# Third block of a four-block transformer: routing each token to two of four experts by an on-chip sort

## The chip, the cores and the metric

The kernel runs on one core of a Trainium2 chip. The metric is the device time of one execution in microseconds (us); 1322.86 us is the median of three runs before the change. Engines are named as the profile names them: PE (TensorE matmuls; PEld its weight loads), DVE (VectorE), ACT (ScalarE), POOL (GpSimd), SP (SyncE, which here only issues DMAs). A line number such as L1105 is a line of the kernel before.

## The reference, cut to what matters

The input is 32 sequences ("batches") of 128 tokens with 144 channels, float32. A transformer block, a rotation per sequence, a second transformer block and a third one follow one another. The third block is attention and then a mixture of four experts, of which each token uses the two with the largest gate logits:

```python
h = _modulate(_ln(x), sh_msa, sc_msa)
...                                                   # attention, 16 heads of 9 channels
x = x + g_msa[:, None, :] * o
xf = _modulate(_ln(x), sh_mlp, sc_mlp).reshape(-1, C)  # 4096 tokens, C = 144
gate_logits = xf @ w_gate                              # 4 experts
topk_logits, topk_idx = jax.lax.top_k(gate_logits, 2)
gates = jax.nn.softmax(topk_logits, axis=-1)
cw = jnp.sum(jax.nn.one_hot(topk_idx, 4) * gates[..., None], axis=1)
hmid = jax.nn.gelu(jnp.einsum('tc,ech->eth', xf, w1) + b1[:, None, :], approximate=True)  # 576 wide
eo = jnp.einsum('eth,ehc->etc', hmid, w2) + b2[:, None, :]
return x + g_mlp[:, None, :] * jnp.einsum('te,etc->tc', cw, eo)
```

## The kernel before

All of x stays in SBUF (`x_sb`). The order of the instructions on every engine is written out by hand. Time is cut into ticks: in each tick one batch of a layer enters its attention, and the main loop at L1344 emits three stages of three neighbouring batches (`scores`, `weigh`, `project_out`) with named gaps "a", "e", "t", "stats", "b0", "b", "den", "pre1", "c", "y1", "y2", "y3", "z", "d" between them. `put(tick, gap, f, ...)` hangs any other work into a gap; `put2` puts the two halves of a generator into two gaps. Batches go in groups of four (G), eight groups per layer; layer l starts at tick first[l] = 0, 35, 67. Each engine executes its instructions in the order in which the loop emitted them, so a gap fixes an instruction's place on its engine.

In the third block, for group n with t0 = 67 + 4n, the layer norm of a batch is transposed by `ln_T` into `hM_m` (128 channels) and `hR_m` (16 channels and a constant, in four copies of 32 rows). `gate_logits` is at tick t0+7; `expert_ranks` and `expert_weights` at t0+8 make `cw`, four weights per token, two of them zero. Then every expert is computed for every token:

- `moe1` (through `fc1` and `both`, matmuls at L665) multiplies the 512 tokens of a group, as the moving operand, by chunks of 128 hidden columns. Two experts are a pair of 9 chunks (`PAIRS`); the last 64 columns of both share chunk `SHARED`. Gelu is at L964, into `hid`.
- `shared_by_gate` (L1093, L1094) multiplies the shared chunk by the two gate weights.
- `moe2_parts` (L1105, L1110) multiplies `hid` of one batch by the second weights, 4 products per batch and expert and one for the shared chunk; L1114 and L1116 on DVE add the result, times the gate weight, to `acc`.
- `moe_bias` (L1076, L1078, on POOL) starts `acc` with the experts' biases; `moe_out` (L1121, L1122, on POOL) multiplies by the gate of the block, adds to `x_sb`, and L1123 stores the group.

A group's experts take ticks t0+8 to t0+12. Attention of the last batch ends with tick 100; what is left of groups 6 and 7 follows it with no attention beside it. Weights of the third block's first pair are loaded once by `load_late`, of the second by the `load_pair` at L1329. SP also loads the gates of each group (L305), several ticks ahead.

Of the kernel before, what the change touches and what calls it, by code (L numbers as in the profile page):

```python
# [8 lines left out]
F32 = mybir.dt.float32  # L9
U32 = mybir.dt.uint32  # L10
I32 = mybir.dt.int32
# [17 lines left out]
PAIR_COLS = NPC * (256 + C)  # L29
# [3 lines left out]
NG = B // G  # L33
EPS = 1e-6
# [32 lines left out]
def tile_kernel(ctx: ExitStack, tc: tile.TileContext, a: dict, out: bass.AP):  # L67
# [43 lines left out]
    hid = const.tile([128, NPC, G, T], F32, name="hid")  # L111
    prep = ExitStack()
# [906 lines left out]

    def gate_logits(g):  # L1020
# [13 lines left out]
    def expert_ranks(g):  # L1034
# [5 lines left out]
        cw = small.tile(sh, F32, tag="cw", name=f"cw_{g[1]}", bufs=2)  # L1040
# [11 lines left out]
        nc.vector.tensor_scalar(rank, rank, 1.5, None, ALU.is_lt)  # L1052
# [4 lines left out]
    def expert_weights(g):  # L1057
        lg, (cw, rank, one) = gr[g].pop("lg"), gr[g]["cw"]
        nc.scalar.activation(lg, lg, AF.Exp)
        nc.vector.tensor_tensor(cw, lg, rank, ALU.mult)  # L1060
        nc.vector.tensor_reduce(one, cw, AX.X, ALU.add)
        nc.vector.reciprocal(one, one)
        nc.vector.tensor_tensor(cw, cw, one.to_broadcast([128, G, E]), ALU.mult)
        gr[g]["cw"] = cw

    def moe_bias(g, i):

        if i == 0:
            gr[g]["acc"] = late.tile([128, G, C], F32, tag="acc", name=f"acc_{g[1]}", bufs=2)
        acc = gr[g]["acc"][:, i, :]  # L1070
        for e in range(E):
            w = gr[g]["cw"][:, i, e : e + 1]
            t = acc
            if e:
                t = late.tile([128, C], F32, tag="bias", name=f"bias_{g[1]}_{i}_{e}", bufs=2)
            nc.gpsimd.tensor_scalar(t, L3.b2[:, e, :], w, 0.0, ALU.mult, ALU.add)  # L1076
            if e:
                nc.gpsimd.tensor_tensor(acc, acc, t, ALU.add)  # L1078

    def moe1(g, pair, part, rest_first):  # L1080
        to = ((0, 1, 2), (SHARED, 3, 4), (5, 6, 7))[part]
        return fc1(g, PAIRS[pair], f"3_{g[1]}_{pair}", 3 * part, to, rest_first)

    def shared_by_gate(g, pair):


        cwx = late.tile([128, G, 2, 64], F32, tag="cwx", name=f"cwx_{g[1]}_{pair}", bufs=1)
        cw = gr[g]["cw"][:, :, 2 * pair : 2 * pair + 2]
        nc.gpsimd.tensor_copy(cwx, cw.unsqueeze(3).to_broadcast([128, G, 2, 64]))
        yield  # L1090
# [5 lines left out]
    def moe2(g, e, i):  # L1096
        for _ in moe2_parts(g, e, i):
            pass
# [456 lines left out]
```

## Time and profile before

| | |
|---|---|
| three runs | 1322.86, 1318.93, 1335.67 us |
| profiled execution | 1327.05 us, its span 1325.3 us |
| granted PE clock | 0.991 of full |
| busy in the span | PE 1266.7, ACT 832.9, DVE 799.8, POOL 699.9 us |
| tick 75, the first with expert work (batch 6 in `weigh`) | 841.8 us |
| last projection of attention (`project_out` of the last batch) | issued at 1250.3 us, done by 1250.9 us |
| last matmul of the experts ends / store issued / span ends | 1318.7 / 1322.0 / 1325.3 us |

A row of the list of groups reads: line, engine, operation, output<-input by the program's names, shapes, count | busy us, mean ns of one | idle time of that engine just before them and what ended it. A row of windows gives start:end, length and then each engine's busy time with the number of instructions. The chain of waits lists start, us, and the piece of work that the end waited for. A float32 product appears as two matmul passes (a single 128x128 transpose as one). The times of the profile are those of one execution; 1322.86 is the median of the others.

### The profile page before, as it was taken

The page shows a single profiled execution, that of the slowest core. Times are in us where ns is not written, and L with a number is a line of the kernel's source. Part 1 is how long each engine was busy: PE and PEld are TensorE (multiplying, and loading weights), DVE is VectorE, ACT ScalarE, POOL GpSimd, SP SyncE. Part 2 cuts the span into 40 slices and gives each one's busy share as a digit, 9 for nine tenths or more (in the row PEclk, how much of TensorE's full clock was granted, in tenths as well). Part 3 has the DMA queues.
Part 4 walks back from the last instruction along what each step waited for, and adds up shares of the span by engine and source line. Part 5 has one row for each costly group of instructions (what it writes and reads, how often), then busy time and mean ns, then how long its engine had stood idle before and what let it go on. Part 6 is the DMA issues. An engine that isn't in the chain of part 4 may idle for free.

```text
span 1325.3 us, 35652 instructions
## 1 busy us (share of the span) xinstructions
PE 1266.7 (96%) x14180; PEld 923.5 (70%) x14180; DVE 799.8 (60%) x2516; ACT 832.9 (63%) x1832; POOL 699.9 (53%) x1691
## 2 busy tenths in 40 slices
PE   6989898999999989999999999999999999999997
PEld 5668686786776566677776766667676767677665
DVE  5698988866764355666566667545454546455322
ACT  2568767678767555686767777756565656555431
POOL 5667777756744343445445445736363636351632
PEclk9999999999999999999999999999999999999999
DMA  9200000000003000000110000201000000000000
GB/s 229 61 2 21 20 3 18 20 3 22 20 13 121 18 11 20 11 20 10 45 29 14 17 20 11 75 11 19 10 19 11 19 11 19 10 19 2 19 9 9
DMA packets 21671, 34.43 MB, mean 26 GB/s; under 512 B 2304, under 2 KB 12448, under 8 KB 21248
## 3 DMA queue, kind: packets, MB, share of 16 engines
q1 hardware_dynamic: 20848, 31.70, 8.0%
q8 instruction: 114, 1.87, 0.6%
q10 hardware_dynamic: 656, 0.42, 0.2%
q14 instruction: 53, 0.43, 0.1%
HBM read 29.65 MB, written 2.47 MB: 24 GB/s over the span
## 4 chain that ended last, share of the span: by engine, by line
PE 69%; DVE 4%; ACT 1%; issue 1%; POOL 0%; POOLq 0%; DVEq 0%
PE ps_h L665 19%; PE ps_f L1105 9%; PE ps_s L853 6%; PE ps_qk L665 6%; PE ps_o L880 5%; PE ps_w L853 5%; PE ps_f L970 4%; PE ps_pj L944 3%; PE ps_v L665 2%; DVE nm L858 2%; PE ps_f L1110 1%; PE ps_o L812 1%; PE ps_cw L1093 1%; PE ps_hT_m L652 1%; PE ps_hT_m L653 1%; PE ps_z L1002 1%
## 5 line engine op out<-in xcount | busy, mean ns | idle before, releaser
L858 DVE TENSOR_REDUCE nm<-ps_s 128x4 f32<-128x512 f32 x384 | 246.4, 682 | 96.9 <-PE ps_w L853 79.3
L865 ACT ACTIVATE pr<-ps_w 128x512 f32<-128x512 f32 x384 | 208.6, 595 | 107.6 <-PE ps_w L853 106.0
L853 PE MATMUL ps_w<-q,kT 32*128 32x128 f32 x3072 | 228.6, 283 | 0.2 <-ACT hid L964 0.2
L853 PE MATMUL ps_s<-kT,qT 32*128 32x256 f32 x1536 | 227.9, 404 | 0.7 <-ACT kT L788 0.6
L853 PEld LDWEIGHTS ps_w<-q,kT 32*128 32x128 f32 x3072 | 193.3, 186 | 9.7 <-issue 6.2
L964 ACT ACTIVATE hid<-ps_h 128x512 f32<-128x512 f32 (+1 forms) x224 | 119.1, 591 | 108.9 <-PE ps_h L665 108.5
L853 PEld LDWEIGHTS ps_s<-kT,qT 32*128 32x128 f32 x1536 | 134.9, 184 | 30.0 <-issue 9.2
L665 PE MATMUL ps_h<-hM_m,mlps 128*128 128x512 f32 x304 | 146.3, 615 | 0.0
L1114 DVE SCALAR_TENSOR_TENSOR acc<-ps_f,cw,acc 128x144 f32<-128x144 f32 x128 | 46.6, 366 | 152.3 <-PE ps_f L1110 73.6
L930 POOL TENSOR_TENSOR x_sb<-x_sb,res_a 128x144 f32<-128x144 f32 x96 | 47.0, 489 | 151.2 <-DVE res_a L933 149.9
L880 PE MATMUL ps_o<-pr,vaug 128*32 128x128 f32 x3072 | 104.9, 277 | 0.8 <-issue 0.8
L880 PEld LDWEIGHTS ps_o<-pr,vaug 128*32 128x32 f32 x3072 | 78.7, 110 | 34.3 <-PE ps_w L853 20.0
L665 PEld LDWEIGHTS ps_h<-hM_m,mlps 128*128 128x128 f32 x304 | 53.9, 191 | 66.2 <-issue 65.0
L731 POOL TENSOR_SCALAR kT<-kT,cst 128x512 f32<-128x512 f32 x40 | 62.3, 1563 | 61.6 <-ACT kT L718 60.6
L970 PE MATMUL ps_f<-mlps,hid 128*128 128x144 f32 x640 | 93.2, 293 | 0.0
L970 PEld LDWEIGHTS ps_f<-mlps,hid 128*128 128x128 f32 x640 | 82.5, 191 | 7.3 <-issue 3.4
L865 ACT ACT_TABLE_LOAD x57 | 73.1, 1283 | 8.0 <-PE ps_w L853 7.2
L626 POOL TENSOR_SCALAR rs_m_a<-mv_m_a 128x2 f32<-128x2 f32 x81 | 15.5, 191 | 116.6 <-DVE mv_m_a L624 88.2
L655 ACT ACTIVATE hM_m<-ps_hT_m,modM 128x128 f32<-128x128 f32 x96 | 44.6, 465 | 49.1 <-PE ps_hT_m L653 49.0
L961 ACT ACT_TABLE_LOAD x58 | 74.4, 1283 | 1.0
L930 POOL TENSOR_TENSOR x_sb<-x_sb,res_m 128x144 f32<-128x144 f32 x64 | 32.3, 510 | 80.0 <-DVE res_m L933 79.9
L1105 PEld LDWEIGHTS ps_f<-pair,hid 128*128 128x128 f32 x512 | 66.9, 190 | 8.4 <-issue 7.7
(324 smaller groups left out, 2963.5 us busy)
## 6 DMA issues: line engine op xcount, KB each, us to landing
gates<-gates SPq DMA_DIRECT2D x48, 288.0 KB, 3.5
x_sb<-in_x SPq DMA_DIRECT2D x8, 288.0 KB, 9.4
out_x<-x_sb SPq DMA_DIRECT2D x8, 288.0 KB, 2.5
mlps<-in_L_mlp SPq DMA_DIRECT2D x2, 1000.0 KB, 6.1
pair<-in_L_mlp SPq DMA_DIRECT2D x1, 1800.0 KB, 9.5
mlps<-in_L_mlp SPq DMA_DIRECT2D x1, 1800.0 KB, 8.2
pow<-in_W SPq DMA_DIRECT2D x4, 320.0 KB, 7.7
mlps<-in_L_wmod SPq DMA_DIRECT2D x4, 290.0 KB, 4.9
```

The lines of the kernel that those rows point to most:

```text
L665: nc.tensor.matmul(ps, x, y, start=k == 0, stop=k == 1)
L731: eng.tensor_scalar(o, k, m, None, ALU.mult)
L853: nc.tensor.matmul(o, x, y, start=True, stop=True)
L858: nc.vector.tensor_reduce(nmv[:, at0 : at0 + 2, ONE : ONE + 2], view.rearrange("p (r t k) -> p r t k", t=2, k=T), AX.X, ALU.max, negate=True,)
L865: nc.scalar.activation(pr[:, 4 * e : 4 * e + 4, :].rearrange("p s q -> p (s q)"), view, AF.Exp, scale=SCALE,)
L880: nc.tensor.matmul(po[rows4(j), t, :], v[:, 4 * j + 2 * t + r, :], prs[j // 2][:, 4 * (j % 2) + 2 * r + t, :], start=r == 0, stop=r == 1,)
L930: nc.gpsimd.tensor_tensor(x_sb[:, b, :], x_sb[:, b, :], t, ALU.add)
L961: nc.scalar.activation(t, half, AF.Gelu_apprx_tanh)
L964: nc.scalar.activation(hid[:n, i], ps[:n], AF.Gelu_apprx_tanh)
L970: nc.tensor.matmul(ps, hid[:, at0, i, :], w2[:, m, :], start=m == 0, stop=m == NFC - 1)
L1105: nc.tensor.matmul(ps[:, 0, :], hid[:, at0 + m, i, :], w2[:, at0 + m, :], start=m == 0, stop=m == 3)
L1114: nc.vector.scalar_tensor_tensor(acc, ps[:, 0, :], w, acc, ALU.mult, ALU.add)
```

## The change

Each token's normalised row is written to DRAM, a sort on the chip gives every (token, choice) pair a slot in tiles of 128 slots, each tile belonging to one expert, and only these tiles are multiplied. Groups are sorted in five sets of 1, 1, 2, 2 and 2 groups (`SETS`). A set of one group has 11 tiles, of two groups 19: twice its number of batches, and 3 for the tiles that experts fill only in part. The count is fixed, whatever the routing: 79 tiles in all, in 42 pairs (37 of two tiles, 5 of one).

- `token_rows`: two transposes, a DVE copy and a store of 128 rows of 1 KB to `sets[k].x`, for each batch.
- `places`: counts, offsets and slot numbers, in steps that are put into the gaps of one tick: DVE instructions with matmuls between them, ending in `S.expert` (a tile's expert), `S.take` (token of each slot) and `S.give` (where its result goes). Slots without a token go to a dump area.
- `fetch`: an indirect DMA on POOL gathers the 128 rows of a tile. `fetch_w`: SP reads the tile's expert into a register and loads that expert's first weights and the last 64 rows of the second with three DMAs from a computed address.
- `turned`, `expert1`, `expert2`: transposes of the gathered rows, the first product with gelu, the second product. In `expert2` PE reads the expert into a register and takes the second weights, as the moving operand, from a computed address in `exp_w2` (four experts, loaded once).
- `give`: an indirect DMA on POOL scatters a tile's 128 result rows of 576 B to `sets[k].y`. `fetch_y` loads both results of every token of a batch; `combine` weighs and adds them (DVE), multiplies by the gate and adds to `x_sb` (POOL), and stores two batches.
- `put_sets` replaces the placing of `moe1`, `moe2` and the rest: set k is sorted at tick ready, and its first ("f") and second ("s") products go one after the other into three slots per tick ("b0", "pre1", "y2"), stretched over the ticks until the next set begins; the last set has one unit per slot from tick 105.

Gone are `moe_bias`, `shared_by_gate`, `moe1`, `moe2_parts`, `moe_out` and the loads of the pairs. The gate logits and the ranking stay, with a few more DVE instructions. The core of the diff:

```diff
+SETS = ((0,), (1,), (2, 3), (4, 5), (6, 7))
...
+    row_bufs = [hid_flat[:, 2304 + 256 * i : 2560 + 256 * i] for i in range(3)]
+    xg_bufs = [hid_flat[:, 3072 + 256 * i : 3328 + 256 * i] for i in range(6)]
+    h_bufs = [hid_flat[:, 1152 * i : 1152 * i + 1152] for i in range(2)]
...
+    def token_rows(s):
+        layer, b, g, i = of(s)
+        k, j = set_of[g[1]]
+        ps = bank([128, 2, 128], f"ps_row_{s}")
+        nc.tensor.transpose(ps[:, 0, :], gr[g]["hM_m"][:, i, :], ident)
+        nc.tensor.transpose(ps[:, 1, :], gr[g]["hR_m"][:, i, :], ident)
+        row = row_bufs[b % 3]
+        nc.vector.tensor_copy(row, ps.rearrange("p a c -> p (a c)"))
+        at0 = (j * G + i) * T
+        nc.sync.dma_start(sets[k].x[at0 : at0 + T], row)
...
-    def moe_bias(g, i):
-        if i == 0:
-            gr[g]["acc"] = late.tile([128, G, C], F32, tag="acc", name=f"acc_{g[1]}", bufs=2)
-        acc = gr[g]["acc"][:, i, :]
...
+    def places(k):
+        S = sets[k]
+        nb, nt = S.nb, S.nt
+        ps = bank([128, 9, E], f"ps_pre_{k}")
+        nc.tensor.matmul(ps[:, : nb + 1], K.lower, S.sel[:, : nb + 1], start=True, stop=False)
+        ones = cst[:, K_ONES : K_ONES + 1].to_broadcast([128, 128])
+        for b in range(nb):
+            nc.tensor.matmul(
+                ps[:, b + 1 : nb + 1], ones,
+                S.sel[:, b : b + 1].to_broadcast([128, nb - b, E]), start=False, stop=b == nb - 1,
+            )
...
+        for q in range(nb // 2):
+            hot = work.tile([128, 4, 128], F32, tag=("xM", "xR")[q % 2], name=f"hot_{k}_{q}", bufs=1)
+            ps = bank([128, 19], f"ps_slots_{k}_{q}")[:, :nt]
+            for i in range(4):
+                at0 = 4 * q + i
+                nc.vector.tensor_scalar(
+                    hot[:, i], K.iota, hilo[:, 1, at0 : at0 + 1], None, ALU.is_equal
+                )
+            for i in range(4):
+                nc.tensor.matmul(ps, hot[:, i], tv[:, 4 * q + i], start=i == 0, stop=i == 3)
...
+    def fetch(k, t):
+        S = sets[k]
...
+        S.xg[t] = xg_bufs[n_taken["x"] % 6]
...
+        nc.gpsimd.indirect_dma_start(
+            S.xg[t], None, S.x[:, :],
+            bass.IndirectOffsetOnAxis(ap=S.take[:, t : t + 1].bitcast(U32), axis=0),
+        )
+    def fetch_w(k, j):
+        S = sets[k]
...
+        slot = mlps[:, 3 * FF * (n % 2) : 3 * FF * (n % 2 + 1)]
+        half_ = mlps[:, 6 * FF + C * (n % 3) : 6 * FF + C * (n % 3 + 1)]
+        S.w1[j] = slot, half_
+        for u, t in enumerate(tiles_of(k, j)):
+            e = nc.values_load(
+                S.expert[:, t : t + 1], engines=(mybir.EngineType.SP,), min_val=0, max_val=E - 1
+            )
+            rows = slice(64 * u, 64 * u + 64)
+            nc.sync.dma_start(
+                slot[:, FF * u : FF * u + FF], a["L3_w1"][bass.ds(e * 128, 128), :]
+            )
+            nc.sync.dma_start(
+                slot[rows4(u), 2 * FF : 3 * FF], a["L3_w1R"][bass.ds(e * 32, 32), :]
+            )
+            nc.sync.dma_start(half_[rows], a["L3_w2h"][bass.ds(e * 64, 64), :])
+    def turned(k, j):
+        S = sets[k]
+        n = len(tiles_of(k, j))
+        ps = bank([128, 4, 128], f"ps_X_{k}_{j}")
+        for u, t in enumerate(tiles_of(k, j)):
+            x = S.xg.pop(t)
+            nc.tensor.transpose(ps[:, 2 * u], x[:, :128], ident)
+            nc.tensor.transpose(ps[:, 2 * u + 1], x[:, 128:], ident)
+        S.xT = late.tile([128, 4, 128], F32, tag="xT", name=f"xT_{k}_{j}", bufs=1)
+        nc.scalar.copy(S.xT[:, : 2 * n], ps[:, : 2 * n])
+    def expert1(k, j):
+        S, xT = sets[k], sets[k].xT
+        ts = list(enumerate(tiles_of(k, j)))
+        slot, half_ = S.w1.pop(j)
+        psa = [bank([128, 4, 128], f"ps_H_{k}_{t}") for u, t in ts]
+        psc = bank([128, 128], f"ps_Hc_{k}_{j}")
+        for u, t in ts:
+            for m in range(4):
+                at0 = FF * u + 128 * m
+                nc.tensor.matmul(
+                    psa[u][:, m], slot[:, at0 : at0 + 128], xT[:, 2 * u], start=m == 0, stop=False
+                )
+        for u, t in ts:
+            at0 = FF * u + 512
...
+        for m in range(5):
+            at0 = 2 * FF + 128 * m
+            for u, t in ts:
+                rows = rows4(u)
+                o, n = (psa[u][:, m], 128) if m < 4 else (psc[64 * u : 64 * u + 64], 64)
+                nc.tensor.matmul(
+                    o, slot[rows, at0 : at0 + n], xT[rows, 2 * u + 1], start=False, stop=m >= 3
+                )
...
+        for u, t in ts:
+            nc.scalar.activation(
+                H[:, 512 * u : 512 * u + 512], psa[u].rearrange("p m t -> p (m t)"),
+                AF.Gelu_apprx_tanh,
+            )
...
+    def expert2(job):
+        k, j, half_, H, ts = job
+        S = sets[k]
+        at = [
+            nc.values_load(
+                S.expert[:, t : t + 1], engines=(mybir.EngineType.PE,), min_val=0,
+                max_val=E - 1,
+            ) * EXP2_COLS
+            for u, t in ts
+        ]
+        ps = [bank([128, C], f"ps_Y_{k}_{t}") for u, t in ts]
+        def w(at0, u):
+            return exp_w2[:, at0 : at0 + (E - 1) * EXP2_COLS + C][:, bass.ds(at[u], C)]
+        for u, t in ts:
+            for m in range(4):
+                at0 = 512 * u + 128 * m
+                nc.tensor.matmul(
+                    ps[u], H[:, at0 : at0 + 128], w(C * m, u), start=m == 0, stop=False
+                )
+        for u, t in ts:
+            rows = slice(64 * u, 64 * u + 64)
+            nc.tensor.matmul(ps[u], H[rows, 1024:1152], half_[rows], start=False, stop=True)
...
+        for u, t in ts:
+            nc.vector.tensor_copy(y[:, u], ps[u])
+        for u, t in ts:
+            to_give.append((k, t, y, u))
...
+    def give():
...
+        nc.gpsimd.indirect_dma_start(
+            S.y[:, :], bass.IndirectOffsetOnAxis(ap=S.give[:, t : t + 1].bitcast(U32), axis=0),
+            y[:, u], None,
+        )
+    def fetch_y(s):
...
+        y = work.tile([128, 2, C], F32, tag="qkraw", name=f"y_{s}")
+        nc.sync.dma_start(
...
+    def combine(g, i0):
+        cwT, n = gr[g]["cwT"], g[1]
+        k, j = set_of[n]
+        S = sets[k]
+        ps = [bank([128, C], f"ps_b2_{n}_{i0 + i}") for i in range(2)]
+        for i in range(2):
+            rows = slice(32 * (i0 + i), 32 * (i0 + i) + E)
+            nc.tensor.matmul(ps[i], cwT[rows], b2[rows], start=True, stop=True)
+        for i in range(2):
+            s = 2 * B + n * G + i0 + i
+            b, at0 = n * G + i0 + i, j * G + i0 + i
...
+            nc.vector.scalar_tensor_tensor(
+                acc, acc, S.w[:, at0, 0:1], ps[i], ALU.mult, ALU.add
+            )
+            nc.vector.scalar_tensor_tensor(
+                acc, y[:, 1], S.w[:, at0, 1:2], acc, ALU.mult, ALU.add
+            )
+            nc.gpsimd.tensor_tensor(acc, acc, gr[g]["gm"][:, i0 + i, :], ALU.mult)
+            nc.gpsimd.tensor_tensor(x_sb[:, b, :], x_sb[:, b, :], acc, ALU.add)
+        b = n * G + i0
+        nc.sync.dma_start(out[b : b + 2].rearrange("b t c -> t b c"), x_sb[:, b : b + 2, :])
...
-                for pair in range(2):
-                    at_ = t0 + 8 + 2 * pair
-                    put2(at_, "stats", "b0", moe1, g, pair, 0, True)
-                    put2(at_, "den", "pre1", moe1, g, pair, 1, False)
-                    put2(at_ + 1, "stats", "b0", moe1, g, pair, 2, True)
-                    put2(at_, "stats", "y1", shared_by_gate, g, pair)
-                    put2(at_, "y2", "y3", moe2_parts, g, 2 * pair, 0)
-                    put(at_ + 1, "b", moe2, g, 2 * pair, 1)
-                    put(at_ + 1, "c", moe2, g, 2 * pair, 2)
-                    put(at_ + 1, "y2", moe2, g, 2 * pair, 3)
-                    for i in range(G):
-                        put(at_ + 2, "aabb"[i], moe2, g, 2 * pair + 1, i)
...
+    units = []
+    for k, ns in enumerate(SETS):
+        ready = first[2] + G * ns[-1] + 8
+        end = first[2] + G * SETS[k + 1][-1] + 10 if k + 1 < len(SETS) else None
+        nt = 2 * G * len(ns) + 3
+        pairs = (nt + 1) // 2
+        units.append((ready, end, nt, pairs))
...
+        for k, (ready, end, nt, pairs) in enumerate(units):
+            for gap in ("b0", "pre1") + ("c", "y2") * (G * len(SETS[k]) // 4) + ("z",):
+                put(ready, gap, lambda k=k: sets[k].steps())
+            mine = [u for u in order if pairs_[u[1]][0] == k]
+            q0 = max(q, len(SLOTS) * (ready + 2))
+            room = None if end is None else len(SLOTS) * end - q0
+            for i, u in enumerate(mine):
+                q = when[u] = q0 + (i if room is None else i * room // len(mine))
...
+        for u in order:
+            J, at_ = u[1], when[u]
+            k, j = pairs_[J]
+            if u[0] == "f":
+                if J == 0:
+                    put(*slot_of(at_ - 1), turned, k, j)
+                put(*slot_of(at_), first_product, J)
+                if J + 1 < len(pairs_):
+                    put(*slot_of(max(at_, when["f", J + 1] - 1)), turned, *pairs_[J + 1])
+            else:
+                put(*slot_of(at_), lambda J=J: expert2(jobs.pop(J)))
+                for i in range(1, 3):
+                    put(*slot_of(at_ + i), give)
+                if J + 3 < len(pairs_):
+                    fetches(J + 3, at_)
+                if j == units[k][3] - 1:
+                    done = at_ // len(SLOTS) + 2
+                    for i, nn in enumerate(SETS[k]):
+                        g = 2, nn
+                        put(done + i, "den", gate_bias, g)
+                        for i0 in (0, 2):
+                            for ii in range(2):
+                                put(done + i, ("b", "y1")[i0 // 2], fetch_y, 2 * B + nn * G + i0 + ii)
+                            put(done + i, ("c", "z")[i0 // 2], combine, g, i0)
+                        need_gm[done + i - 1].append(nn)
...
```

## The prediction

> **What bounds the kernel now.** The page's busy times were read first, then busy time by windows, then the chain of waits in one group of the third block, then its end. The windows run from tick 75 (first expert work) to the last projection of attention, and from there to the last matmul; the columns are start:end, length, busy PE, PEld, DVE, ACT, POOL, clock, DMA.
>
> ```profile
> PE 1266.7 (96%) x14180; PEld 923.5 (70%) x14180; DVE 799.8 (60%) x2516; ACT 832.9 (63%) x1832; POOL 699.9 (53%) x1691
> ...
> 841.80:1250.90 409.10, 408.65 (x3908) 290.39 (x3906) 210.28 (x631) 239.15 (x453) 210.26 (x428) 1.00 0.06 17
> 1250.90:1318.70 67.80, 67.72 (x389) 45.52 (x387) 18.84 (x61) 20.36 (x44) 20.53 (x44) 1.00 0.02 5
> ...
> 957.00:1022.50 65.50, 65.50 (x633) 46.54 (x637) 34.17 (x104) 38.85 (x75) 34.67 (x69) 1.00 0.05 15
> ```
>
> PE has no gap in either stretch; 65.5 us is one group, four ticks. So the third block lasts as long as PE's work: what leaves PE is gained, and any new wait of PE costs in full. The chain within that group gives the shares, and pieces of it give prices:
>
> ```profile
> 958.00 2.77 PE ps_h L665 x6
> 960.77 0.98 PE ps_f L1105 x8
> ...
> 1264.37 0.11 PE ps_hT_m L652
> ...
> 1238.13 0.88 PE ps_w L853 x16
> ```
>
> A float32 product is two passes. A pass of 512 columns is 2.77/6 = 0.46 us, of 144 columns 0.98/8 = 0.122, of 128 columns 0.11; where two products use different 32-row strips they run side by side, 0.88/16 = 0.055 a pass. In the group's chain the experts hold 32.9% (ps_h) + 24.6% + 3.2% (ps_f, L1105 and L1110) + 1.8% (ps_cw) = 62.5%, 40.9 us; eight groups make 327 us, of which 68 lie after attention and 259 before. Attention and the rest are 24.6 us a group.
>
> **PE's work after.** First product of a pair of tiles: 16 passes x 0.11 = 1.76, the half chunk 4 x 0.055 (two column halves) = 0.22, the 16 extra channels 20 x 0.055 = 1.10; transposes 4 x 0.11 = 0.44; second product 16 x 0.122 + 0.25 = 2.21. That is 5.73 us a pair; a lone tile, without a neighbour, 3.65. 37 and 5 of them: 230 us. `token_rows` 64 x 0.11 = 7; sorts (25 products for a two-group set, 13 for one group, two passes each at about 0.1) 3 x 5 + 2 x 2.6 = 20; biases 5. Sum 262 against 327: only 65 us less, since 128 full tile products became 79, but small moving operands and extra work take part of it back.
>
> Where it lies decides. By tick 100 `put_sets` has emitted sets 0 to 2 (65 + 55 us) and ten of the twenty units of set 3 (30), with rows 7, sorts 15 and biases 3: 175 us against 259, **-84** before the end of attention. The other 87 us come after it, where 68 were.
>
> **What is added to PE before attention ends.** Ticks 75 and 76 lose their filler, since set 0 starts at 77: attention alone is 6.15 us, but neighbouring ticks of the second block are never below 8.0 apart: **+4**.
>
> `expert2` reads two registers and computes eight addresses on PE's sequencer. One such load is in the trace:
>
> ```profile
> L585 SPq TENSOR_LOAD <-more x1: 500/500/500, 246.7 to 246.7; - x1
> L585 SPq FUSED_REGOPS  x1: 188/188/188, 247.3 to 247.3; - x1
> L585 SPq SEQ_ASSERT  x1: 29/29/29, 247.5 to 247.5; - x1
> L585 PEldq TENSOR_LOAD <-more x1: 488/488/488, 318.9 to 318.9; - x1
> ```
>
> Two loads with their register steps are 2 x (0.49 + 0.19 + 0.03) = 1.42 us, eight addresses 8 x 0.19 = 1.52: 2.94 us a pair when nothing hides it. But the load at 318.9 ran while matmuls in front of it started as late as 322.0: the sequencer was 3 us ahead, which would hide it all. PE's semaphore steps in the third block stand 0 to 3 us ahead of their matmuls, with 0.65 in the middle. So 0 to 2.94; I take **0.8** a pair, nearer to hidden: 26 second products, +21.
>
> Sort steps put DVE work and the matmuls that need it into one gap: 12 such steps for sets 0 to 3. PE waits while DVE finishes two score reductions (0.68 each, L858) and four one-hot rows (about 0.25 each), 2.4 us if bare; half of it is taken: 15. The bias products share banks with DVE work that waits for `fetch_y`: 8 times about 1.2, 10. Bounds 0 and 50; **+25**.
>
> POOL: of its 34.7 us a group, the expert work is 16 x 0.39 + 12 x 0.49 (L1076, L1078) + 1.2 + 2.9 = 16; that goes. `combine` adds 8 x 0.49. Then 9.9 gathers and 9.9 scatters a group, of which no row exists. Nearest rows: SP's plain DMA issue, 0.39, and POOL's own longest operation, 1.56 (L731).
>
> ```profile
> L1123 SPq DMA_DIRECT2D out_x<-x_sb x8: 388/389/389, 915.1 to 1322.0; - x8
> ...
> DMA to landing us min/median/max: 2.4/2.5/3.1
> ...
> L731 POOL TENSOR_SCALAR kT<-kT,cst 128x512 f32<-128x512 f32 x40 | 62.3, 1563 | 61.6 <-ACT kT L718 60.6
> ```
>
> I take c = 1.3, nearer to the latter, because 128 rows have to be addressed one by one: POOL 22.3 + 19.8 x 1.3 = 48 us of a group that lasts about 60. Hidden, but the layer norms queue behind gathers and scatters on POOL, and their transposes on PE are late: **+10** (0 to 80, see the rival). ACT stays near 40 us a group (fewer columns of gelu, one more copy a pair), DVE near 35; both hidden. SP moves some 400 KB a tile, 4 MB a group: in 60 us that is below what the first slices of the page show (229 GB/s).
>
> Sum before attention ends: -84 + 4 + 21 + 25 + 10 = **-24**.
>
> **The end.** Before, 1250.9 to 1325.3 is 74.4 us: 67.8 of packed matmuls, DVE 0.4, POOL 1.40 + 1.39, the store and its landing. After, three parts.
>
> First, the rest of set 3: 25 us of products, sort 5, logits 1, registers 5, so 36. Meanwhile the last group passes through norm, row store (2.5), logits, ranks, the whole sort (some 25 small DVE steps at 0.2, 16 one-hot rows) and the first gather (1.3 + 2.5) before its first product can start: about 34 us in series. Both are in the same in-order queues and don't overlap perfectly: 45.
>
> Second, set 4, one unit per slot with nothing beside it: 55 + 8 for registers = 63. Here the order of the built program adds a wait: each scatter waits until the scatter before it into the same DRAM tile has landed, and POOL stands still meanwhile, with the next gathers behind it. Two scatters a pair are 2 x (1.3 + 2.5) = 7.6 us against PE's 6.5: about 8 in all. SP issues six loads a pair, 2 x (0.72 + 3 x (0.19 + 0.39)) = 4.9 us and some 3 to landing, into two slots used in turn: a load has from one first product to the next but one, about 9 us, and just fits. Those that stand on SP behind the stores of set 3, which wait for POOL, come late: 4. Sum 75 (55 to 100).
>
> Third, the close: copy 0.3, last scatter 3.8, then four rounds, because on SP each store stands in front of the next `fetch_y`: load 3.0, DVE 2 x 0.37, POOL 4 x 0.49 = 5.7 each; last store 2.9. Sum 30, where 6 were.
>
> 45 + 75 + 30 = 150, **+76**. Net -24 + 76 = **+52** on 1325.3. The profiled execution, 1327.05, stands 4.2 over the median, so the forecast is 1322.9 + 52 = 1375 us.
>
> [...]
>
> ```profile
> 450.00:460.00 10.00, 8.81 (x59) 5.23 (x60) 3.41 (x8) 3.94 (x7) 1.88 (x9) 0.83 0.00 0
> ...
> 451.19 0.36 PE L812 MATMUL ps_nm<-cst,nm 128*128 128x128 f32 x1 [1.38 <-DVE nm L858]
> ```
>
> The granted clock sank to a mean of 0.83 after an idle stretch of only 1.38 us. [...]
>
> **Rivals.** *The work is hidden after all (faster).* One mechanism: PE's sequencer and queues run far enough ahead. For it: PE busy for 408.65 of 409.10 us, the 3 us lead at L585. Against: the end has nothing to hide behind. Without registers (-34), sort waits (-25), POOL lateness (-10), and with an end whose parts overlap (-22), it is 1284. It passes below 1296 once these exposures stay under about 12 us of my 91. *POOL becomes the bound.* At c above (60 - 22.3)/19.8 = 1.9 us POOL outlasts PE. At 2.5 a group takes 72: +74 - 10, and 2 x 5.0 a pair in the end, +26: 1465. For it: serial scatters; against: longest POOL row 1.56. *Registers bare.* 2.94 instead of 0.8 a pair: 42 x 2.1 = +88: 1463. For it: eight computed addresses in 2 us of matmul; against: the lead.
>
> **How the numbers follow.** Forecast 0.48 (its own range 1325 to 1425), hidden 0.26, POOL 0.13, registers 0.13. The range reaches to both sides' bounds, 1290 to 1460. Two per cent, about what a measurement can tell from no change, is 1296 to 1349: from hidden 0.20 faster and 0.06 same, from the forecast 0.07 same; the rest slower.
>
> **What would show it.** Right: groups of about 60 us, attention ending some 25 us earlier, 140 to 160 us after it. PE gaps before ps_Y name the registers, before ps_slots the sort, before ps_X and xT POOL. Wrong: an end under 110 us, or POOL over 90% busy beside attention.

## The result, and the profile after

The changed kernel takes 1560.35 us (median of three runs, 1558.56 to 1561.08) where the kernel before takes 1322.86: 1.177 times as long, 95% interval 1.164 to 1.189. Forecast were 1375 us in a range of 1290 to 1460. The sign was right, the size was not: +237 us for +52.

Line numbers are now those of the changed kernel; lines that the change did not touch stand 3 higher than before (L880 is L883). First the page of the changed kernel: busy times, then the rows of busy tenths and of the granted PE clock in 40 slices.

```profile
PE 1353.9 (87%) x15254; PEld 1052.8 (68%) x15254; DVE 823.0 (53%) x2697; ACT 824.5 (53%) x1849; POOL 765.9 (49%) x1666
...
PE   6999989998999899999997788797889879788881
...
PEclk9999999999999999999998797897888968886885
```

From slice 22 on, in the third block, the clock is no longer 9 but between 5 and 9, and PE is mostly at 7 or 8 tenths. Busy time by windows shows it in numbers: from tick 75 to the last projection of attention, from there to the last product of the experts, and the close (start:end, length, busy PE, PEld, DVE, ACT, POOL, clock, DMA).

```profile
841.30:1357.10 515.80, 424.56 (x4386) 346.22 (x4382) 220.60 (x749) 221.57 (x433) 224.27 (x348) 0.85 0.28 82
1357.10:1521.90 164.80, 135.60 (x964) 115.27 (x963) 25.98 (x107) 30.45 (x79) 64.27 (x79) 0.79 0.40 117
1521.90:1558.70 36.80, 2.72 (x19) 1.40 (x18) 6.02 (x17) 0.53 (x2) 10.82 (x21) 0.55 0.19 54
```

Tick 75 starts where it did (841.3 for 841.8), so the whole loss lies behind it: 717.4 us where 483.5 were. The stretch with attention grew from 409 to 516, the rest from 74 to 202. PE was busy for 563 us of it, more than before (476), but at a clock of 0.85, 0.79 and 0.55.

That asks for a split in three. The trace gives the stretches in which the granted clock was one half. Busy time with its share in such stretches counted half is PE's work at full clock; the other half of that share is the loss by the clock; the rest is idle. This is worked out from the trace for each profiled execution, from tick 75 to the end of the span:

| | length | work at full clock | loss by the clock | idle |
|---|---|---|---|---|
| before | 483.5 | 476.4 | 0.0 | 7.2 |
| after | 717.4 | 472.8 | 90.0 | 154.5 |
| difference | +233.9 | -3.6 | +90.0 | +147.3 |
| forecast, in the same terms | +52 | -65 | 0 | +117 |

So the forecast missed three things: 61 us of work that was not saved, 90 us of slow clock, 30 us of idle time. What PE waited for in that stretch, by the list of waits (engine, line waited for: us in all, times, longest):

```profile
PE ps_X L1264 <- DMA hid<-expert_x,take: 29.6, 13, 6.4
PE ps_cwT L1368 <- POOL cw_rows L1366: 26.2, 5, 10.8
PE ps_slots L1205 <- DVE hot L1201: 23.8, 16, 7.5
PE ps_o L815 <- DVE nm L861: 14.2, 5, 7.7
PE ps_s L856 <- POOL kT L734: 8.1, 4, 3.9
PE ps_Y L1327 <- issue: 7.5, 10, 1.2
```

Gathered rows, the copy of the expert weights on POOL (L1366, in `gate_bias`), the sort's one-hot rows, and then attention's own inputs, which come late because DVE and POOL are behind. The row of the registers (`ps_Y`, "issue") is the smallest of these six; with all other causes PE stands 14.7 us in front of `ps_Y`. One sort tick shows how a wait costs twice. The four windows are: before the wait, the wait, what follows it, the recovery.

```profile
1068.00:1072.40 4.40, 4.37 (x47) 3.43 (x47) 3.89 (x21) 1.94 (x4) 3.85 (x8) 1.00 0.00 0
1072.40:1076.90 4.50, 0.04 (x1) 0.07 (x1) 4.07 (x14) 1.32 (x3) 0.00 (x0) 0.81 0.16 47
1076.90:1092.30 15.40, 13.41 (x56) 12.39 (x56) 4.20 (x23) 0.00 (x0) 0.00 (x0) 0.50 0.00 1
1092.30:1100.00 7.70, 7.70 (x115) 6.43 (x113) 5.25 (x22) 2.85 (x7) 2.88 (x8) 1.00 0.09 24
```

The timeline names the wait that ends at 1076.9 (start, us, engine, line, and in brackets the idle time before it):

```profile
1076.86 1.86 PE L1205 MATMUL ps_slots<-tv,hot 128*128 128x19 f32 x8 [4.48 <-DVE hot L1201]
```

PE stands for 4.5 us while DVE works for 4.07 us through small steps of `places`, four steps of attention, two score reductions and the four one-hot rows; then it computes for 15.4 us at half clock, which costs another 7. POOL does nothing in that time: its next addition (L933) waits for DVE, and DVE for PE's projection.

### The profile page after: what moved, and what is told of

Read it like the earlier page. It is cut to its first block, busy times and chain, and to the rows that moved or that the text cites. A ratio compares the mean times of both kernels' runs of the same rounds, so it can differ in the third digit from the quotient of the medians.

```text
span 1558.7 us, 40096 instructions
## 1 busy us (share of the span) xinstructions
PE 1353.9 (87%) x15254; PEld 1052.8 (68%) x15254; DVE 823.0 (53%) x2697; ACT 824.5 (53%) x1849; POOL 765.9 (49%) x1666
## 5 line engine op out<-in xcount | busy, mean ns | idle before, releaser
L856 PE MATMUL ps_w<-q,kT 32*128 32x128 f32 x3072 | 243.9, 294 | 0.2 <-ACT hid L967 0.2
L856 PE MATMUL ps_s<-kT,qT 32*128 32x256 f32 x1536 | 232.4, 420 | 8.9 <-POOL kT L734 8.1
L856 PEld LDWEIGHTS ps_w<-q,kT 32*128 32x128 f32 x3072 | 203.5, 196 | 4.1 <-DVE res_a L936 0.7
L856 PEld LDWEIGHTS ps_s<-kT,qT 32*128 32x128 f32 x1536 | 135.9, 193 | 42.9 <-issue 11.7
L933 POOL TENSOR_TENSOR x_sb<-x_sb,res_a 128x144 f32<-128x144 f32 x96 | 47.0, 490 | 196.4 <-DVE res_a L936 195.2
L1346 POOL DMA_INDIRECT expert_y<-ys,give x79 | 80.4, 1017 | 120.9 <-DMA expert_y<-ys,give 43.9
L1301 ACT ACTIVATE hid<-ps_H 128x512 f32<-128x512 f32 x79 | 43.1, 594 | 168.5 <-PE ps_H L1293 122.5
L1335 DVE COPY ys<-ps_Y 128x144 f32<-128x144 f32 x79 | 21.0, 303 | 198.4 <-PE ps_Y L1332 176.7
L1327 PE MATMUL ps_Y<-exp_w,hid 128*128 x632 | 108.5, 335 | 14.7 <-issue 7.5
L1327 PEld LDWEIGHTS ps_Y<-exp_w,hid 128*128 128x128 f32 x632 | 99.6, 229 | 21.9 <-issue 11.5
L883 PE MATMUL ps_o<-pr,vaug 128*32 128x128 f32 x3072 | 111.1, 287 | 1.2 <-issue 1.2
L1279 PE MATMUL ps_H<-xT,mlps 128*128 128x128 f32 x632 | 89.9, 300 | 8.2 <-ACT xT L1267 5.9
L883 PEld LDWEIGHTS ps_o<-pr,vaug 128*32 128x32 f32 x3072 | 82.9, 114 | 20.5 <-issue 8.9
L1279 PEld LDWEIGHTS ps_H<-xT,mlps 128*128 128x128 f32 x632 | 82.5, 210 | 15.8 <-ACT xT L1267 6.8
L1232 POOL DMA_INDIRECT hid<-expert_x,take x79 | 77.9, 986 | 28.1 <-issue 27.0
L658 ACT ACTIVATE hM_m<-ps_hT_m,modM 128x128 f32<-128x128 f32 x96 | 44.6, 465 | 79.4 <-PE ps_hT_m L656 75.7
L668 PE MATMUL ps_h<-hM_m,mlps 128*128 128x512 f32 x160 | 77.7, 617 | 0.0
L734 POOL TENSOR_SCALAR kT<-kT,cst 128x512 f32<-128x512 f32 x40 | 62.6, 1568 | 29.6 <-ACT kT L721 28.4
```

What stands on the lines that cost most here:

```text
L668: nc.tensor.matmul(ps, x, y, start=k == 0, stop=k == 1)
L734: eng.tensor_scalar(o, k, m, None, ALU.mult)
L856: nc.tensor.matmul(o, x, y, start=True, stop=True)
L883: nc.tensor.matmul(po[rows4(j), t, :], v[:, 4 * j + 2 * t + r, :], prs[j // 2][:, 4 * (j % 2) + 2 * r + t, :], start=r == 0, stop=r == 1,)
L933: nc.gpsimd.tensor_tensor(x_sb[:, b, :], x_sb[:, b, :], t, ALU.add)
L1232: nc.gpsimd.indirect_dma_start(S.xg[t], None, S.x[:, :], bass.IndirectOffsetOnAxis(ap=S.take[:, t : t + 1].bitcast(U32), axis=0),)
```

## The experiments

The runs stand in three groups of four; each group ran on one chip, beside runs of the kernel before. The changed kernel took 1560 us when it was first measured, 1536 in the second group and 1563 in the third, while the kernel before took 1323, 1327 and 1335; so a run is compared with the changed kernel of its own group. The first group has none; there the comparison is with 1563 us, because the kernel without the sort ran both in that group (1490) and in the third (1485). The split of the profiled executions, from tick 75 on, as above:

| run | median, us | against after | ratio to before, 95% | length | work | clock | idle |
|---|---|---|---|---|---|---|---|
| e3_warm | 1550.2 | -13 | 1.161 to 1.170 | 706.8 | 528.3 | 64.7 | 113.8 |
| e10_less_pe | 1523.4 | -40 | 1.141 to 1.152 | 677.9 | 418.8 | 79.6 | 179.5 |
| e6_no_sort | 1489.8 | -73 | 1.114 to 1.123 | 641.8 | 452.5 | 56.6 | 132.7 |
| e4_fixed_w2 | 1554.6 | -8 | 1.161 to 1.171 | 705.5 | 471.7 | 90.2 | 143.6 |
| e0_after_again | 1536.2 | | 1.146 to 1.160 | 690.0 | 472.1 | 79.4 | 138.5 |
| e1_bias_early | 1531.8 | -4 | 1.145 to 1.158 | 685.9 | 473.0 | 76.8 | 136.1 |
| e5_no_reload | 1531.3 | -5 | 1.146 to 1.159 | 673.7 | 473.0 | 64.8 | 135.9 |
| e7_scatter | 1537.0 | +1 | 1.150 to 1.165 | 665.5 | 472.6 | 66.1 | 126.7 |
| e0_after_third | 1563.0 | | 1.164 to 1.181 | 707.1 | 475.9 | 80.1 | 151.0 |
| e6_no_sort_again | 1485.1 | -78 | 1.109 to 1.124 | 642.4 | 451.6 | 54.9 | 135.9 |
| e9_combo | 1450.4 | -113 | 1.080 to 1.097 | 599.6 | 476.0 | 43.5 | 80.1 |
| e11_floor | 1410.0 | -153 | 1.052 to 1.067 | 558.4 | 451.5 | 24.3 | 82.7 |

In the unchanged kernel and in e1, e5, e7 and e9, which compute the same products, the work comes out at 472 to 476 us while the loss by the clock runs from 43 to 90; so counting the share at half clock by half is right.

Two cautions. Ahead of tick 75 the code is nearly the same in all, yet that stretch takes between 837.7 and 854.0 us in these profiles (861.4 in e7, see there), and the medians contain it. And the profiled executions of e5 and e7 were the shortest of their runs.

**Is the slow clock a cause or a symptom?** Useless products are put in front of the waits.

```diff
+    def warm(n):
+        for i in range(n):
+            t = bank([128, 512], "ps_warm")
+            nc.tensor.matmul(t, ident, exp_w2[:, :512], start=True, stop=True)
...                                     # before the first slot product of a sort
+            warm(3 if q == 0 else 0)
...                                     # before the first transposes of a set
+        warm(5 if j == 0 else 0)
...                                     # before the transpose of the expert weights
+        warm(2)
```

> The changed kernel with useless products of 128x512 added on PE, whose result nobody reads: 3 before the first slot product of each sort, 5 before the first transposes of each set, 2 before each transpose of the expert weights, 56 in all (112 passes, some 26 us at 0.46 us for 512 columns and two passes each 52 us). They stand in front of the waits named in the trace of the changed kernel (gaps of 7.5, 6.4, 4.9, 4.5, 5.1 and 7.6 us). Theory CLOCK (254.8 us of the 717.4 after 841.3 run at half clock, each time after a stretch of 3.4 us that PE spent partly idle, which costs some 90 us): the added work fills gaps that last anyway and keeps the clock up; about 110 us of half clock go, worth 40, and some 12 us of added work come out of its gap: 20 to 45 us LESS than the 1560 of the changed kernel, and the mean granted clock rises from 0.911 to 0.94 or more. Rival, the clock is only a symptom (the waits set the pace and PE would be idle anyway): 0 to 20 us MORE, by what of the added work is not covered.

Some 55 us of useless work cost no time. The median is 13 us below the yardstick, but that is not clearly a gain: from tick 75 on the profile is 11 us shorter than the first one of the changed kernel (717.4) and no shorter than that of the third group (707.1). Against these two, work rose by 52 to 56, idle time fell by 37 to 41 and the loss by the clock by 15 to 25. So the clock is a cause: without its share the added work would have cost 15 us by either comparison. The mean granted clock rose to between 0.926 and 0.941 in the four executions (0.941 in the profiled one), where the eleven of the changed kernel have 0.901 to 0.921. The 20 to 45 us of the expectation were not reached, since 171 of 255 us of half clock stayed. Of the 21 falls that are left, nine still follow a gap in front of the slot products or the weight transposes, where products had been added; the rest follow other gaps.

**Does PE's own work still bound it?** The 20 short products of a pair are left out.

```diff
-        for m in range(5):
+        for m in range(0):
...                                     # L1293, with stop= moved to the products before it
```

> The changed kernel without the 20 short products of each pair that add the last 16 channels and the bias to the first product (L1293); this part of the computation is left out. In the trace of the changed kernel they take 65.8 us of PE. Theory PE (PE's own work still bounds the third block, 563 us busy of 717; its passes turned out longer than forecast, 0.122 for 0.11 and 0.076 for 0.055): 45 to 75 us less than 1560. Rival TRANSFER (gathers, scatters and weight loads set the pace of the pairs): less than 25 us less, PE only waits longer.

54 us of work went, about 40 us of time by the medians (29 to 40 from tick 75 on, against the two profiles): idle time rose by 25 to 28. That is under the expected 45, and over the 25 that the rival allows. Work is bounding, but a part of what PE no longer computes it waits: the wait for gathers alone grew from 29.6 to 37.5 us.

**The sort.**

```diff
-            gen = places(k)
-            S.steps = lambda gen=gen: next(gen, None)
+            f = fx[:, :33] if S.nt == 11 else fx[:, 33:]     # table, loaded once
+            f = f.rearrange("p (c t) -> p c t", c=3)
+            S.take, S.give, S.expert = f[:, 0], f[:, 1], f[:1, 2]
+            S.steps = lambda: None
```

> The changed kernel without the sort: the token of each slot, its destination and the expert of each tile come from a table loaded once (equal shares of the experts, every real slot full), so the routing of the tokens is left out; ranks, weights, gathers, scatters and all products stay. Theory SERIAL (the sort's small products stand in PE's queue in front of ready work, wait there for DVE and bring the clock down): gaps before L1205 and L1138 (25.6 us) go, their work (25 us at full clock), and the half clock that stands at the sorts (some 75 us low, worth 30): 65 to 100 us less than 1560. The forecast's own terms for the sort (20 of products, 15 of waits, some 20 in the end): 55 less. Rival GATHER (the first gather of each set takes the sort's place as what PE waits for): 35 less or still smaller.

> The kernel without the sort once more (fixed table of slots and experts; the routing is left out), now beside the changed kernel on the same chip. Theory SERIAL: 60 to 85 us less than the changed kernel of this call. Rival GATHER: 35 less or still smaller.

73 us in the first group and 78 in the group with its own yardstick, both in the theory's range and far from the rival's. Of the 75 us between that pair of profiles 11 lie ahead of tick 75, where the sort has no part; so it costs some 65. The split of these is the lesson: 24 us of work, 25 us of clock, but only 15 us of idle time. The sort's own gaps (23.4 us) vanished, and others grew in their place:

```profile
PE ps_cwT L1372 <- POOL cw_rows L1370: 35.0, 6, 10.8
PE ps_X L1268 <- DMA hid<-expert_x,fixed: 28.4, 11, 6.4
PE ps_o L815 <- DVE nm L861: 16.7, 6, 6.9
```

**The registers.**

```diff
-        at = [nc.values_load(S.expert[:, t : t + 1], ...) * EXP2_COLS for u, t in ts]
+        at = [t % E * EXP2_COLS for u, t in ts]
```

> The changed kernel with the second weights of a tile taken from a fixed address (tile number modulo 4) in place of one computed from a register on PE; the choice of the expert in the second product is left out. Theory SERIAL/CLOCK: only the 14.7 us of idle time before L1327 and the slower passes (0.134 for 0.126, 632 of them, 5 us) belong to the registers: 12 to 35 us less than 1560. Rival REGISTERS (2.94 us a pair, nothing hidden, as priced in the prediction): 100 us less or more.

About 8 us by the medians, 2 to 12 from tick 75 on against the two profiles: at most 0.3 us a pair, at or under the lower end of the 12 to 35 expected. The 14.7 us in front of `ps_Y` are gone, but those in front of `ps_X` rose from 32.5 to 40.6. Within a run of equal passes the starts stayed 0.123 us apart, so the register address does not slow a product. Registers as the bound are out.

**Weight loads, scatters, and the transpose of the expert weights.** The second group, beside the changed kernel:

> The changed kernel unchanged, on the chip of the next three runs, as their yardstick. Every theory expects what was measured: 1555 to 1570 us, 715 to 720 us from tick 75 to the end of the span.

```diff
 e1_bias_early
-                        put(done + i, "den", gate_bias, g)
+                put(t0 + 9, "den", gate_bias, g)             # and four buffers for cwT
 e5_no_reload
         S.w1[j] = slot, half_
+        if n > 2:
+            return
 e7_scatter
-            S.y[:, :], bass.IndirectOffsetOnAxis(...)
+            S.y[t % 4][:, :], bass.IndirectOffsetOnAxis(...)  # four DRAM tiles
```

> The changed kernel with `gate_bias` (POOL copy, PE transpose, ACT copy) put one tick after the weights of its group are made, in four buffers, where it stood behind the scatters of its set's last pair. Theory SERIAL: PE waits 32.6 us in front of this transpose, each time because the POOL copy stands behind indirect DMAs that themselves wait; moved, the copy finds POOL free: 20 to 40 us less than 1560, a part of it through the clock (four falls begin at these gaps). Rival CLOSE (the last 18 us of these gaps lie in the close, where PE's wait is not what sets the end but the last scatter, the load of the results and POOL's multiplications): 5 to 15 less. Rival of no effect (the next products wait for the same POOL queue anyway): within 5.

> The changed kernel with the first weights fetched for the first three pairs only and these buffers used for all 42, so 39 of 42 fetches with their register loads on SP and some 30 MB of traffic are gone; the choice of the expert in the first product is left out. Theory SERIAL/CLOCK: PE waits 10.4 us in front of ps_H and ps_Hc in all, partly for these loads: 5 to 20 us less than 1560. Rival TRANSFER (the weight loads crowd out the gathers, the scatters and the loads of results, whose landings PE and DVE wait for): 40 to 80 less.

> The changed kernel with the scatters of a set spread over four DRAM tiles in turn, so that a scatter waits for the fourth before it and no longer for the one before it; the results are then read from one of the four, so three quarters of them are left out (that tile is filled once before, long before tick 75). Theory SERIAL/CLOCK: POOL's waits for the scatter before (43.9 us, 27.7 of them after attention) lie mostly beside PE's work; they reach PE through the gathers and the copy of `gate_bias` behind them: 5 to 20 us less than 1560. The prediction's own term, some 1.5 us a pair in the end: 15 less. Rival SCATTER (POOL's queue is what the pairs of the last set wait for: 9.6 us a pair): 30 less or more.

By the medians all three lie within 5 us, which these runs cannot tell from nothing. For e1 and e5 that is the answer: the theory's 20 to 40 us for the early transpose was wrong, and the 30 MB of weight traffic do not set the pace.

For e7 it is not. Filling its extra tile makes DVE wait for that transfer, and PE for DVE, once and long before tick 75; the changed kernel has no such wait (list of waits of PE up to 845 us):

```profile
PE ps_s L856 <- DVE x_sb L1021: 16.1, 1, 16.1
```

So the median, 1 us more, hides some 15 us less behind tick 75 (24 less in the profile, 665.5 for 690.0, but that execution was the shortest). This estimate meets the theory's 5 to 20 and the 15 of the prediction's own term; the 30 or more of the rival are not reached. That scatters wait for one another costs some time, then, but does not set the pace.

Why the early transpose gained nothing is told by the list of waits. In the changed kernel of that group (list of waits of PE):

```profile
PE ps_cwT L1368 <- POOL cw_rows L1366: 32.2, 6, 10.6
PE ps_X L1264 <- DMA hid<-expert_x,take: 31.0, 12, 6.2
```

and with the transpose moved early:

```profile
PE ps_cwT L1368 <- POOL cw_rows L1366: 28.7, 7, 5.6
...
PE ps_X L1264 <- DMA hid<-expert_x,take: 9.7, 8, 2.0
```

The new place stands in front of the first gather's transposes. Ahead of the close, some 20 us left the wait for gathers and some 15 came up at the copy; in the close, the 18.3 us in front of the transpose became 10.9 in front of L1381 and 9.5 more behind PE's last product. In all, idle time fell by 2.4 us. This fits DVE and POOL being some 5 us behind PE at that place (the longest waits are 6.2 and 5.6 us), which PE pays at whichever wait it meets first; no run shows that by itself.

**Moving everything that waits.** This version computes everything:

```diff
-            for gap in ("b0", "pre1") + ("c", "y2") * (G * len(SETS[k]) // 4) + ("z",):
-                put(ready, gap, lambda k=k: sets[k].steps())
+            two = len(SETS[k]) == 2                            # the sort over two ticks
+            where = [(0, "b0"), (0, "y2")]
+            where += [(1, g_) for g_ in (("a", "b", "den", "c") if two else ("a", "b"))]
+            where += [(1, "c")]
...                                     # in places(): one-hot rows a step ahead
+            if q + 1 < nb // 2:
+                hot_rows(q + 1)
+            hot = hots.pop(q)
...                                     # first products four slots later
-            q0 = max(q, len(SLOTS) * (ready + 2))
+            q0 = max(q, len(SLOTS) * (ready + 2) + 4)
...                                     # weights written by DVE where PE transposes them
+        cw = K.cw[g[1] % 2][:, :, :E]
...                                     # last set: all eight loads of results together
+                                if k == len(SETS) - 1:
+                                    at = done, "b"
```

> The changed kernel unchanged, the yardstick of the other three runs of this call, since it took 1560 us on one chip and 1536 on another while the kernel before took 1323 and 1327. Every theory expects 1530 to 1565 us.

> A version that computes everything and only moves what waits: the sort is spread over two ticks with each quarter of the one-hot rows made on DVE one step ahead of its products on PE; the first products of a set begin four slots later, so that the first gathers have landed; the expert weights are written by DVE straight into the tile that PE transposes (no POOL copy) and transposed one tick after they are made; the eight loads of results of the last set are issued together, ahead of its stores. Theory SERIAL/CLOCK: of 138 us of idle PE in front of sort (23.5), first gather (31) and weight transpose (32) some 60 go, the half clock behind them (some 100 us low) gives 35, the close about 10: 70 to 110 us less than the changed kernel of this call. Rival MOVED (the run with the weight transposes moved early gained 4 us only: the same lateness of DVE and POOL met PE at the next wait): 15 to 45 less.

113 us less than the changed kernel beside it, a little over the expected 110: from tick 75 on 71 of idle time, 37 of clock, no work. The wait for the sort's rows is gone from the list, that for gathers is down to 8.0 us, and the close took 25.4 us for 36 (the loads of its four rounds now go out together):

```profile
844.30:1263.60 419.30, 381.86 (x4287) 310.47 (x4284) 219.69 (x743) 223.84 (x433) 219.43 (x333) 0.93 0.34 96
1263.60:1418.50 154.90, 135.88 (x1070) 114.69 (x1069) 27.16 (x113) 33.29 (x85) 71.16 (x88) 0.86 0.48 138
1418.50:1443.90 25.40, 1.79 (x17) 1.22 (x16) 7.60 (x17) 0.00 (x0) 10.38 (x19) 0.56 0.27 78
```

The waits do go when the producers get time, all of them together; what each of the four changes gives by itself is not shown. It is still 1.088 times the kernel before (1.080 to 1.097).

**What is left with every suspect off.** No sort, no registers, three weight fetches, no POOL copy, products two slots later, by the edits above.

> All suspects off at once: no sort (fixed table), second weights from a fixed address, first weights fetched for three pairs only, expert weights without the POOL copy and transposed early, first products two slots later. The routing and the choice of experts are left out; every product, gather and scatter stays. Theory PE (the products themselves need as much PE time as the dense experts did: 450 us at full clock from tick 75, where the kernel before needs 476 in a span of 483): 110 to 150 us less than the changed kernel of this call, and still 50 or more above the kernel before. Rival of the forecast (the products need 412 us with the sort, some 390 without it, and what lies between is waits): at or below the kernel before.

153 us less, just over the expected 110 to 150, and 75 above the kernel before; so the forecast's rival is out. PE's work at full clock is 451.5 us in it, against 476 in the kernel before: with the sort taken out altogether, the tiles need only 25 us of PE less than all four experts for every token. The versions that sort and compute everything need 472 to 476 us of PE, no less than the kernel before, which stands idle for only 7. So a better placing of the same products could at best draw level, and the close speaks against that (25 us in the best version, 7 before). This follows from the split; no run shows it.

## Why the prediction was wrong, point by point

Three terms of the sum fell short: the work of PE by 61 us, the clock by 90, the waits by 30.

**PE's work (forecast -65, measured -4).** The first step that failed is the price of a pair: 5.73 us there, 7.04 in the trace at full clock (278 us for 79 tiles; 230 were forecast). First product 3.84 for 3.08, transposes 0.60 for 0.44, second product 2.61 for 2.21. One first product at full clock and without a wait (start, us from the first start to the last end, line, shapes, count), up to the transposes of the next pair:

```profile
1114.25 2.05 PE L1279 MATMUL ps_H<-xT,mlps 128*128 128x128 f32 x16
1116.23 0.44 PE L1284 MATMUL ps_Hc<-xT,mlps 128*64 128x128 f32 x4
1116.60 1.16 PE L1293 MATMUL ps_H<-xT,mlps 32*128 32x128 f32 x16
1117.69 0.43 PE L1293 MATMUL ps_Hc<-xT,mlps 32*64 32x128 f32 x4
1118.06 0.33 PE L1264 MATMUL ps_X<-cst,hid 128*128 128x128 f32 x1
```

From 1114.25 to 1118.06 it takes 3.81 us. Inside a run of equal passes the prices were right: starts of L1279 lie 0.112 us apart, also from one tile to the other, of L1327 0.123, and two passes on different strips of L1293 take 0.112 together. But where the shape of the product changes, from row to row above, the first step or two take about 0.2 us, and the new products change often; of the steps of L1293 every tenth takes 0.20 or 0.21. The kernel before had 512-column passes (0.46 us each) and fewer such changes: after tick 75, 202 passes of its experts stand behind a pass of another shape in the trace, and 273 in that of the changed kernel. Sorts took 25.5 us (20 forecast), row transposes 9.5 (7), biases 9 (5). The statement "128 full tile products became 79" was true and worth nothing.

**The clock (forecast 0, measured 90).** The second step that failed, and the largest: the prediction had the row, a mean clock of 0.83 after 1.38 us of idle time, and gave the clock no term in the sum. There were 26 falls after tick 75, 255 us at half clock in all. The steps that were priced as waits (sort, gather, POOL) each had to carry a second price, about 60% of the wait on average (90 for 154).

**Waits beside attention (forecast 60, measured 91).** The registers were overpriced: 8.5 us stand in front of `ps_Y`, not 21. Sort and biases were near (29 in front of `ps_slots` and `ps_cwT` for 25). What was left out is the first gather of each set, which `put_sets` places one slot ahead of its transposes: 24 us at `ps_X`, 21.6 of them for the gathered rows. It was counted for the last set alone. And DVE and POOL lateness at L815 and L856 is 22 us for 10.

**The end (forecast 150, measured 202).** Idle time after attention was 63 us as forecast (150 less 87 of work), though not in all its parts: 6 us at `ps_Y` where 13 were forecast for registers. Work was 109, and the clock took 30. The close's rounds are 5.9 us each for 5.7. Scatters were overpriced at 3.8 us: in the last pairs, those that wait for one another start 3.0 us apart (1519.18, 1522.21, 1525.23), and the chain that ended last has

```profile
1528.30 2.27 DMA expert_y<-ys,give
```

from issue to landing.

**The rivals.** None came true. POOL as the bound: c was taken as 1.3 us, with 1.9 as the point from which it decides; the page gives 1.0 (columns: busy us, mean ns, idle before and what ended it), and POOL is 49% busy.

```profile
L1346 POOL DMA_INDIRECT expert_y<-ys,give x79 | 80.4, 1017 | 120.9 <-DMA expert_y<-ys,give 43.9
...
L1232 POOL DMA_INDIRECT hid<-expert_x,take x79 | 77.9, 986 | 28.1 <-issue 27.0
```

Registers: the load on PE's weight queue takes 0.30 us, not 0.49, and cost PE at most the 14.7 us in front of `ps_Y`, where the forecast had 34 for all pairs. Hidden work: refuted by the end (202 us, not under 110), as the prediction had argued. All rivals were about who waits; none was about the price of the products or the clock, and these two made 150 of the 181 us by which the forecast missed the profiled span.

What stays open: why the changed kernel is 25 us apart between groups (1536 where 1555 to 1570 were expected). From tick 75 on, the first profile and that of the second group differ by 16 us of idle time (half of it at L815, 14.2 for 6.1) and 11 of clock, with the same work; no run tells more.

## What to carry to other kernels

Price a restructured product by runs of equal passes plus a charge for every change of shape (here about 0.1 us for each of the first steps), and check that sum against the old one before counting tiles. On an engine that is full and in order, count each new wait twice, once as idle time and once as slow clock behind it (here 90 us for 154). A wait that is moved alone can come back under another name (here the transpose moved early, 4 us less); give the late producers time, and move all that hangs on them together (here 113 us less).

## What the runs showed of the hardware

In the profiled execution of the changed kernel the clock's falls and returns stand on a grid of 3.413 us (its 31 falls fit it to within 1%). Five of its cells around one fall:

```profile
1167.25:1170.66 3.41, 3.41 (x45) 2.96 (x44) 2.00 (x6) 0.08 (x1) 2.80 (x3) 1.00 0.71 201
1170.66:1174.08 3.42, 1.79 (x17) 1.47 (x18) 1.85 (x6) 2.37 (x3) 0.10 (x1) 1.00 0.52 162
1174.08:1177.49 3.41, 3.41 (x27) 2.85 (x24) 0.42 (x1) 1.91 (x6) 0.00 (x0) 0.51 0.37 104
1177.49:1180.90 3.41, 3.41 (x40) 2.88 (x43) 0.78 (x2) 2.69 (x6) 0.49 (x1) 0.50 0.01 4
1180.90:1184.32 3.42, 3.23 (x47) 2.78 (x40) 1.59 (x6) 3.01 (x6) 1.47 (x4) 0.99 0.01 2
```

This fall came after a cell with 1.79 us of work, in which a single gap of 1.63 us lay; two cells at half clock followed although PE was busy for 3.41 us of each. In this execution every fall came after a cell in which PE was busy for at most 0.75 of the time, and every return after one busy for 0.94 or more; cells at full clock that were busy for 0.59 to 0.75 went either way. The share of busy time does not tell every fall: in the other profiled executions 15 of 327 falls followed a cell busy for 0.77 or more, and 18 returns one busy for 0.79 to 0.92. The clearest case, in e9, is a fall behind a cell without any idle time:

```profile
1291.88:1295.29 3.41, 3.41 (x40) 2.97 (x37) 0.29 (x3) 2.05 (x4) 0.62 (x1) 1.00 0.56 155
1295.29:1298.70 3.41, 3.41 (x17) 3.41 (x17) 2.25 (x14) 2.48 (x4) 2.31 (x3) 0.50 0.46 154
```

17 of the 31 falls of the changed kernel's execution followed a cell in which PE was busy for 0.43 or more of the time. That helps to explain how 154 us of idle time, 64 of them in gaps shorter than 3.4 us, came with 90 us of loss by the clock.
